# Two attention blocks in fp32 on one core: GpSimd makes two sums of V ahead of its softmax additions

## The chip, the cores and the metric

One NeuronCore of a Trainium2 chip runs the whole program. The metric is the time of one execution on the device in microseconds (us); the median of a few runs is given. A kernel's profile is one further execution under the hardware profiler; its times below are counted from the start of that execution's span.

## The reference

Eight images of 512 channels by 32 x 32 positions pass through two attention blocks, all in float32. Block 0 is a group norm, eight heads of 64 channels, a projection and a residual. Block 1, which the change touches, has one head of 512 channels over 1024 positions:

```python
q = jnp.einsum('oc,bcs->bos', wq, nf) + bq[None, :, None]
k = jnp.einsum('oc,bcs->bos', wk, nf) + bk[None, :, None]
v = jnp.einsum('oc,bcs->bos', wv, nf) + bv[None, :, None]
attn = jnp.einsum('bci,bcj->bij', q, k) * c ** (-0.5)
attn = jax.nn.softmax(attn, axis=-1)
out = jnp.einsum('bcj,bij->bci', v, attn)
out = jnp.einsum('oc,bcs->bos', wo, out) + bo[None, :, None]
return x + out.reshape(b, c, h, w)
```

## The kernel before

The program is one long list of instructions: nothing loops on the chip, and Python unrolls the eight images (`b` = 0 to 7). The order on TensorE (PE), ScalarE (ACT) and VectorE (DVE) is the order of the Python text (`manual_schedule`); the order on GpSimd (POOL) and of the DMAs on SyncE (SP) is chosen by a list scheduler that follows the order of the text as far as operands and buffers let it. Tiles of 128 x 1024 f32 (`tile2`) come from one pool of 36 buffers; a tile takes a buffer that an earlier tile has been done with, and its first writer waits for the last users of that buffer.

Large products are made by Strassen's scheme in Winograd's form. A product of 2 x 2 blocks A and B is done with seven block products of the sums S1 to S4 of A and T1 to T4 of B:

S1 = A21 + A22, S2 = S1 - A11, S3 = A11 - A21, S4 = A12 - S2, and T1 = B12 - B11, T2 = B22 - T1, T3 = B22 - B12, T4 = B21 - T2.

Some block products are themselves split once more in the same way; the tiles named `..._twice` hold the sums of that second step, made by `sums_a` (L477) and `sums_b` (L484).

Block 1 of an image (`attention1`) has these stages on PE:

1. Q (L612), V (L627, L870), with V left in the tiles `c11_v`, `c12_v` (printed as `c_v`).
2. **Phase one of the scores**: `line(0..3)` (L1308) and the split product S1 T1 (L1325).
3. **Phase two of the scores**: the split products A12 B21 and S3 T3, interleaved step by step (L1325). DVE adds each result bank to its tile `p` (L1335, one operand in PSUM and one in SBUF). ACT turns finished tiles into exponentials (L1299). A tile that needs the fifth product gets it by `with_p5` (L1378, DVE, both operands in SBUF, 128 x 1024).
4. **Phase three of the scores**: the split products S4 B22 and A22 T4, in the same way.
5. **The values**: P times V (L1489), in five of seven steps for two groups of channels `c` = 0 and 1, in the order A11, S1, S2, S3, A22; then two split steps (L1619). In the last image all seven steps are whole ones.

The sum of the exponentials over the keys is collected in the tile `acc` by `add_up` (L1294 the first addition, L1296 the others): its half 0 by POOL, its half 1 by DVE. In the values, after the S1 steps, `sums` lets PE multiply both halves of `acc` by ones (L1555); DVE inverts the result (L792), and two small DMAs spread it.

The sums S1 and S2 of V are made by POOL in `sum_v` (L1437): two additions of 128 x 512 each. S3 and S4 of V are made by DVE later. T1 to T4 of P are made by DVE (`finish_values`, L1482, both operands in SBUF). POOL also makes the second-step sums of Q's S4 and A22 (`halve_a`, L477, printed as `S_twice` and `A_twice`), of V's A12 (`halve_v`, L477, `A_v_twice`) and of P's B22 (`halve_p`, L484, `B_p_twice`). In the text, `sum_v(1)` and `sum_v(2)` stand between phase two and phase three.

On DVE the order around the change is: the L1335 additions of phase three, T1 (two instructions), the seven additions of its half of `acc`, T2 (two), S3 of V, T3, the inversion.

Of the kernel before, what the change touches and what calls it, by code (L numbers as in the profile page):

```python
# [65 lines left out]
def two_attention_blocks(  # L66
# [17 lines left out]
    nc = tc.nc  # L84
# [13 lines left out]
    def banks(tag, name):  # L98
        return psum.tile([P, 2, HALF], FP, tag=tag, name=name)

    def tile2(name):
        return tpool.tile([P, 2, HALF], FP, tag="t", name=name)
# [484 lines left out]
    def together(*groups):  # L587

        groups = list(groups)
        spares.clear()  # L590
        while groups:
            for g in list(groups):
                if next(g, g) is g:
                    groups.remove(g)
                else:
                    yield
        spares.clear()

    def at_steps(steps, hooks):

        n = -1
        for n, _ in enumerate(steps):
            for hook in hooks.get(n, []):
                hook()
        assert n >= max(hooks, default=-1)
# [603 lines left out]
    def attention1(xs, norm, b, at_values):  # L1209
# [20 lines left out]
        def halve_a(name, t=None, engine=nc.vector):  # L1230
            q = {f"A{n}": v for n, v in halve(q_parts[name], lambda i, j: (j, i)).items()}
            twice_a[name] = sums_a(q, flat(tile2(f"{name}_twice_{b}")) if t is None else t, engine)
# [55 lines left out]
        def add_up(j, k, i):  # L1288

            engine = nc.vector if i else nc.gpsimd  # L1290
            for u in range(2):
                seen[i].append(ps[j][k][i][:, u, :])
                if len(seen[i]) == 2:
                    engine.tensor_tensor(acc[:, i, :], *seen[i], ALU.add)  # L1294
                elif len(seen[i]) > 2:
                    engine.tensor_tensor(acc[:, i, :], acc[:, i, :], seen[i][-1], ALU.add)  # L1296

        def exp_of(p):
            nc.scalar.activation(p, p, AF.Exp, scale=norm.factor)  # L1299
# [16 lines left out]
        def twice(a, v, tags, i, j, fresh, final):  # L1316

            a, v = twice_a[a], twice_b[v]  # L1320
            line, single = (banks(tag, f"ps_{n}_1_{b}_{i}{j}")[:, 0, :] for tag, n in zip(tags, "ls"))

            def multiply(bank, x, y, start):
                for u in range(2):
                    nc.tensor.matmul(  # L1325
                        bank[:, u * 2 * P : (u + 1) * 2 * P], v[y][:, u * P : (u + 1) * P], a[x],
                        start=start and u == 0, stop=True, skip_group_check=True,
                    )

            def at(r, t):  # L1330
                return ps[j][t][i][:, :, r * 2 * P : (r + 1) * 2 * P]

            def add(bank, r, t):
                bank = bank.rearrange("p (u q) -> p u q", u=2)
                nc.vector.tensor_tensor(at(r, t), bank, at(r, t), ALU.add)  # L1335

            def take(bank, r, t):
                if fresh:
                    nc.scalar.copy(at(r, t), bank.rearrange("p (u q) -> p u q", u=2))
                else:  # L1340
                    add(bank, r, t)

            def done(r, t):
                if final:
                    exp_of(at(r, t))
                    if i == 0 and (r, t) in ((0, 1), (1, 0)):
                        add_up(j, t, i)

            multiply(line, "A11", "B11", True)
            take(line, 0, 0)  # L1350
            yield
            multiply(single, "A12", "B21", True)
            add(single, 0, 0)
            done(0, 0)
            yield
            multiply(line, "S2", "T2", False)
            take(line, 0, 1)
            yield
            multiply(single, "S1", "T1", True)
            take(single, 1, 1)  # L1360
            yield
            multiply(line, "S3", "T3", False)
            add(line, 1, 1)
            done(1, 1)
            yield
            multiply(single, "S4", "B22", False)
            add(single, 0, 1)
            done(0, 1)
            yield
            multiply(line, "A22", "T4", False)  # L1370
            take(line, 1, 0)
            done(1, 0)
            yield

        def with_p5(i, j, k):

            to, other = ps[j][k][i], ps[1][k][1] if i == 0 else ps[0][k][1]
            nc.vector.tensor_tensor(to, to, other, ALU.add)  # L1378

        def c22(k):  # L1380
            with_p5(1, 1, k)
            exp_of(ps[1][k][1])
# [5 lines left out]
        def halve_t3():  # L1388
# [11 lines left out]
        )  # L1400
        halve_a("S4", None, nc.gpsimd)
        halve_a("A22", None, nc.gpsimd)
        at_steps(
            together(
                twice("A12", "B21", "oo", 0, 0, False, True), twice("S3", "T3", "ss", 1, 0, False, False)
            ),
            {3: [lambda: with_p5(0, 1, 1)]},
        )
        c22(0)

        svs = {f"S{n}": tile2(f"s{n}_v_1_{b}") for n in range(1, 5)}
        quarter_v = [
            [[flat(t)[:, i * HALF : (i + 1) * HALF].rearrange("p (u o) -> p u o", u=2) for t in pair]
# [16 lines left out]
        def sum_v(n, engine):  # L1430

            for a, a21 in zip(v_parts, quarter_v[1][1]):
                x, y, op = {
                    1: (a21, a["A22"], ALU.add), 2: (a["S1"], a["A11"], ALU.subtract),
                    3: (a["A11"], a21, ALU.subtract), 4: (a["A12"], a["S2"], ALU.subtract),
                }[n]
                engine.tensor_tensor(a[f"S{n}"], x, y, op)  # L1437


        twice_v, twice_p = {}, {}  # L1440

# [13 lines left out]
            sums = [t[:, i, :].rearrange("p (u q) -> p u q", u=2) for t in ts for i in range(2)]  # L1455
            twice_p[name] = sums_b(q, sums, engine)

        for n in range(1, 3):
            sum_v(n, nc.gpsimd)
        if not last:  # L1460
            halve_v("A12", nc.gpsimd)
        at_steps(
# [202 lines left out]
    with tc.manual_schedule(engines={PE, ACT, DVE}):  # L1665
# [72 lines left out]
        for b in range(B):  # L1738
            if 0 < b < B - 1:
                ahead = [norm0(load_x(b + 1, nc.sync), b + 1)]  # L1740
            xs, norm, qs, ks = layer0(bs, qs, ks, b, ahead[0] if b + 1 < B else None)
            at_values = {}
            if b + 1 < B:

                again, combine_next = ahead[0], Combined(f"again_{b}")

                def load_again():
                    again.xs = load_x(b + 1, nc.sync)

                at_values = {  # L1750
                    2: [load_again], 7: [lambda: again.normed(again.xs, [0], range(NC))],
                    9: [lambda: again.normed(again.xs, [1], range(NC))],
                    10: [lambda: combine_next.take(again.xs)],
                    **{n + 10: [lambda n=n: combine_next.make(n)] for n in range(1, 5)},
                }
                bs = combine_next.parts
            attention1(xs, norm, b, at_values)
# [412 lines left out]
```

## Time and profile before

| | |
|---|---|
| runs | 2862.26, 2857.89, 2862.63 us; median 2862.26 |
| the profiled execution | 2860.0 us, its span 2858.2 us |
| granted TensorE clock, mean | 0.998 |
| PE busy | 2832.0 us (99%) |
| DVE busy | 2141.3 us (75%) |
| ACT busy | 1117.0 us (39%) |
| POOL busy | 282.9 us (10%) in 236 instructions |
| one image | about 352 us |

The span is the time from the first to the last instruction; 1.8 us of the execution lie around it. A busy share is an average over stages that have different limits, and PE's busy time is partly modelled, so what matters for one stage is which wait ends last in it. In the lists of instructions a line gives the start and the duration in us, the engine, the line of the kernel, the operation, the tiles (out<-in) and the shape; xN joins N instructions; in brackets stands the idle time of that engine before it and what ended it. PEld is the weight load that goes ahead of a matmul, PEclk the granted share of PE's full clock.

### The profile page before, as it was taken

To read this page: it belongs to the slowest core of one execution; us is meant where nothing else is said; L and a number is where in the kernel's file an instruction comes from. 1 tells how busy PE (TensorE), PEld (TensorE's weight loads), DVE (VectorE), ACT (ScalarE), POOL (GpSimd) and SP (SyncE) were. 2 spreads that over 40 slices of the span, in tenths; PEclk is the share of its full clock that TensorE was granted. 3 is DMA by queue.
4 is the path that set the end of the run, shared out by engine and by line. 5 is a ranking of instruction groups with operands and counts; after the bars stand their busy time and mean duration, and the time that the engine had idled before them with its cause. 6 is when DMAs were issued, how large, how long until landed. Compare 5 with 4: busy or idle time off the path is not lost.

```text
span 2858.2 us, 38362 instructions
## 1 busy us (share of the span) xinstructions
PE 2832.0 (99%) x15328; PEld 1521.2 (53%) x15328; DVE 2141.3 (75%) x2891; ACT 1117.0 (39%) x1564; POOL 282.9 (10%) x236
## 2 busy tenths in 40 slices
PE   9999999999999999999999999999999999999999
PEld 5434765347643476435763356733567336673365
DVE  6686696867967778776787777777777777767867
ACT  3462324623256232553325522265232642326432
POOL 0000220002100031000400004000040000400012
PEclk9999999999999999999999999999999999999999
DMA  8512132121322212213132131322213222121001
GB/s 287 178 42 74 66 111 93 42 89 53 110 93 49 84 73 93 91 45 107 56 107 76 42 106 56 107 78 47 98 56 107 78 57 87 63 84 58 8 16 38
DMA packets 81227, 228.90 MB, mean 80 GB/s; under 512 B 20080, under 2 KB 20880, under 8 KB 74640
## 3 DMA queue, kind: packets, MB, share of 16 engines
q1 hardware_dynamic: 76576, 210.61, 22.9%
q10 hardware_dynamic: 4464, 15.76, 1.7%
q8 instruction: 122, 2.00, 0.3%
q14 instruction: 65, 0.53, 0.1%
HBM read 157.35 MB, written 30.70 MB: 66 GB/s over the span
## 4 chain that ended last, share of the span: by engine, by line
PE 89%; DVE 9%; SPq 1%; ACT 1%; issue 1%; DMA 0%; POOL 0%; DVEq 0%; POOLq 0%
PE s L921 16%; PE ps_o L940 15%; PE ps_q L612 10%; PE ps_v L627 7%; PE ps_p L612 5%; PE ps_l L1325 5%; PE ps_s L1308 4%; PE ps_s L1325 4%; PE ps_o L1489 3%; PE ps_k L612 3%; PE ps_l_v L627 3%; PE ps_l_qk L849 3%; DVE acc L1296 2%; PE ps_s_v L870 2%; PE ps_s_two L1619 2%; PE ps_s_qk L842 2%
## 5 line engine op out<-in xcount | busy, mean ns | idle before, releaser
L778 ACT ACTIVATE p<-s 128x1024 f32<-128x1024 f32 x512 | 523.6, 1024 | 322.4 <-PE s L921 308.6
L780 DVE TENSOR_TENSOR acc<-acc,p 128x1024 f32<-128x1024 f32 x384 | 469.1, 1222 | 99.5 <-ACT p L778 86.4
L940 PE MATMUL ps_o<-p,v 64*64 64x512 f32 x4096 | 528.7, 589 | 0.0
L940 PEld LDWEIGHTS ps_o<-p,v 64*64 64x64 f32 x4096 | 156.6, 133 | 282.8 <-issue 278.9
L921 PE MATMUL s<-q,k 64*64 64x512 f32 x2304 | 298.5, 591 | 0.0
L921 PE MATMUL s<-c_q,c_k 64*64 64x512 f32 x1792 | 233.0, 590 | 0.0
L339 POOL TENSOR_TENSOR rstd<-rstd,minus_half 128x4 f32<-128x4 f32 (+1 forms) x16 | 19.8, 1239 | 2058.3 <-DVE rstd L338 2058.3
L1489 PE MATMUL ps_o<-t_p,s_v 128*128 128x512 f32 x384 | 171.4, 603 | 4.2 <-ACT held_sum L788 4.2
L921 PEld LDWEIGHTS s<-q,k 64*64 64x64 f32 x2304 | 86.3, 133 | 162.6 <-issue 156.6
L921 PEld LDWEIGHTS s<-c_q,c_k 64*64 64x64 f32 x1792 | 67.7, 133 | 126.3 <-issue 114.9
L780 DVE TENSOR_TENSOR acc<-p,p 128x1024 f32<-128x1024 f32 x64 | 77.8, 1216 | 73.5 <-ACT p L778 73.5
L1299 ACT ACTIVATE p<-p,factor 128x512 f32<-128x512 f32 (+1 forms) x112 | 85.1, 780 | 112.1 <-DVE p L1335 89.6
L1489 PEld LDWEIGHTS ps_o<-t_p,s_v 128*128 128x128 f32 x384 | 73.5, 193 | 98.0 <-issue 85.8
L1313 ACT COPY p<-ps_s 128x512 f32<-128x512 f32 x96 | 53.1, 588 | 178.7 <-PE ps_s L1308 178.7
L1335 DVE TENSOR_TENSOR p<-ps_l,p 128x512 f32<-128x512 f32 x136 | 90.6, 684 | 42.8 <-PE ps_l L1325 41.9
L612 PE MATMUL ps_p<-t_p,w_p 128*128 128x512 f32 x256 | 114.8, 597 | 2.5 <-DVE u_p L1183 1.5
L612 PE MATMUL ps_q<-t,w_wqk 128*128 128x512 f32 x256 | 116.0, 597 | 0.0
L425 ACT COPY u_q<-ps_q 128x512 f32<-128x512 f32 x75 | 43.5, 580 | 177.2 <-PE ps_q L612 177.2
L1066 DVE RECIPROCAL inv<-inv 128x512 f32<-128x512 f32 x28 | 93.7, 3346 | 22.9 <-ACT inv L788 22.9
L425 ACT COPY u_v<-ps_v 128x512 f32<-128x512 f32 x48 | 28.1, 585 | 204.9 <-PE ps_v L627 185.9
L1335 DVE TENSOR_TENSOR p<-ps_s,p 128x512 f32<-128x512 f32 x112 | 74.8, 684 | 41.3 <-PE ps_s L1325 41.3
L627 PE MATMUL ps_v<-w_v,t_again 128*128 128x256 f32 x448 | 99.0, 379 | 0.0
(457 smaller groups left out, 4935.4 us busy)
## 6 DMA issues: line engine op xcount, KB each, us to landing
x<-in_x SPq DMA_DIRECT2D x92, 512.0 KB, 6.8
w_qk<-stored_qk SPq DMA_DIRECT2D x14, 1792.0 KB, 7.2
inv<-inv SPq DMA_DIRECT2D x248, 64.0 KB, 2.0
w_wqk<-stored_wqk SPq DMA_DIRECT2D x8, 1792.0 KB, 7.6
fold<-acc SPq DMA_DIRECT2D x56, 256.0 KB, 3.1
w_wvo<-stored_wvo SPq DMA_DIRECT2D x8, 1792.0 KB, 7.6
out<-x SPq DMA_DIRECT2D x28, 512.0 KB, 3.4
w_v<-stored_v SPq DMA_DIRECT2D x7, 1792.0 KB, 7.1
```

The costliest lines, as they stand in the source:

```text
L612: nc.tensor.matmul(bank, w[a][:, k, c * P : (c + 1) * P], bs[b][:, k, :], start=fresh and k == 0, stop=k == 1, skip_group_check=True,)
L627: nc.tensor.matmul(bank[:, u * 2 * P : (u + 1) * 2 * P], bs[b][:, k, n * P : (n + 1) * P], w[a][:, k, :], start=fresh and u == k == 0, sto ...
L778: nc.scalar.activation(p, s, AF.Exp, scale=factor)
L780: nc.vector.tensor_tensor(acc, first, p, ALU.add)
L849: nc.tensor.matmul(bank, of(i, a)[:, k, :], bs[v][:, k, :], start=start and k == 0, stop=k == 1, skip_group_check=True,)
L921: nc.tensor.matmul(s[cols, j, :], ks[pair][k0 // HALF][rows, k0 % HALF : k0 % HALF + HD], qs[pair][g][rows, :], start=True, stop=True,)
L940: nc.tensor.matmul(o[cols, half, :], vs[kt][rows, c0 : c0 + HD], p[rows, j, :], start=kt == 0, stop=kt == NT - 1,)
L1066: nc.vector.reciprocal(invs[g], invs[g])
L1308: nc.tensor.matmul(bank, bs[v][:, k, t * P : (t + 1) * P], q_parts[a][:, k, :], start=a == "A11" and k == 0, stop=k == 1, skip_group_check ...
L1325: nc.tensor.matmul(bank[:, u * 2 * P : (u + 1) * 2 * P], v[y][:, u * P : (u + 1) * P], a[x], start=start and u == 0, stop=True, skip_group ...
L1335: nc.vector.tensor_tensor(at(r, t), bank, at(r, t), ALU.add)
L1489: nc.tensor.matmul(bank, v_parts[kt // 2][a][:, kt % 2, c * P : (c + 1) * P], p_parts[kt // 2][b][:, kt % 2, cols], start=fresh and kt == ...
```

## The change

The definitions around `sum_v` and the two calls `sum_v(1)`, `sum_v(2)` on GpSimd move from behind phase two to ahead of it. Nothing is computed otherwise, and no instruction is added or removed: 4 GpSimd additions for each image are issued earlier in the text, and the two tiles that they fill take their buffers earlier.

```diff
         halve_a("S4", None, nc.gpsimd)
         halve_a("A22", None, nc.gpsimd)
-        at_steps(
-            together(
-                twice("A12", "B21", "oo", 0, 0, False, True), twice("S3", "T3", "ss", 1, 0, False, False)
-            ),
-            {3: [lambda: with_p5(0, 1, 1)]},
-        )
-        c22(0)
-
         svs = {f"S{n}": tile2(f"s{n}_v_1_{b}") for n in range(1, 5)}
...
                 engine.tensor_tensor(a[f"S{n}"], x, y, op)
 
+        for n in range(1, 3):
+            sum_v(n, nc.gpsimd)
+        at_steps(
+            together(
+                twice("A12", "B21", "oo", 0, 0, False, True), twice("S3", "T3", "ss", 1, 0, False, False)
+            ),
+            {3: [lambda: with_p5(0, 1, 1)]},
+        )
+        c22(0)
+
...
-        for n in range(1, 3):
-            sum_v(n, nc.gpsimd)
         if not last:
             halve_v("A12", nc.gpsimd)
```

## The prediction

> **What bounds the kernel now.** I began with the page: PE is busy 99% of the span, so only a stage where PE waits can give anything. I then took the chain of waits from 360 to 380 us, which is where the moved sums are first used (image 0; the other images show the same at steps of about 352 us).
>
> ```profile
> PE 2832.0 (99%) x15328; PEld 1521.2 (53%) x15328; DVE 2141.3 (75%) x2891; ACT 1117.0 (39%) x1564; POOL 282.9 (10%) x236
> ```
>
> ```profile
> 360.32 1.74 PE ps_l L1325 x8
> ...
> 363.56 3.43 DVE t_p L1482 x2
> 367.00 1.69 DVE acc L1294
> ...
> 375.40 1.65 DVE acc L1296
> ...
> 377.07 0.70 DVE acc L1296
> ...
> 377.82 0.65 PE ps_o L1555 x4
> ```
>
> The chain leaves PE at 362 and runs through DVE until 377.8: T1, then seven additions of 1.65 to 1.69 us, of which only the last takes 0.70. The same addition is slow six times and fast once, so something holds DVE. The instructions of GpSimd and PE in time show what:
>
> ```profile
> 337.55 1.71 POOL L477 TENSOR_TENSOR A_twice<-q,A_twice 128x256 f32<-128x256 f32 x1
> 348.84 1.27 POOL L1294 TENSOR_TENSOR acc<-p 128x512 f32<-128x512 f32 x1 [9.58 <-ACT p L1299]
> 350.07 3.49 POOL L1437 TENSOR_TENSOR s_v<-c_v,c_v 128x512 f32<-128x512 f32 x2
> 353.51 3.57 POOL L1437 TENSOR_TENSOR s_v<-s_v,c_v 128x512 f32<-128x512 f32 x2
> ...
> 369.76 6.73 POOL L1296 TENSOR_TENSOR acc<-acc,p 128x512 f32<-128x512 f32 x4
> ```
>
> ```profile
> 376.54 0.62 PE L1555 MATMUL ps_o<-acc,ones 128*32 128x256 f32 x4 [0.77 <-POOL acc L1296]
> 377.82 0.62 PE L1555 MATMUL ps_o<-acc,ones 128*32 128x256 f32 x4 [0.65 <-DVE acc L1296]
> 379.05 15.67 PE L1489 MATMUL ps_o<-t_p,s_v 128*128 128x512 f32 x32 [0.60 <-ACT held_sum L788]
> ```
>
> POOL stands idle for 9.58 us, then works without a break from 348.84 to 376.49, and DVE becomes fast when POOL stops. PE ends its S1 steps near 375.62 and starts S2 at 379.05: 3.43 us. It waits for POOL's half of acc, for DVE's half, and then for T2. The last wait is put down to ACT, but S2 reads no result of held_sum, and T2's first half on DVE ended at 378.90, so I read it as T2. The last image has no such wait and prices the stage without it:
>
> ```profile
> 2820.89 0.64 PE L1555 MATMUL ps_o<-acc,ones 128*32 128x256 f32 x8
> 2821.45 17.43 PE L1489 MATMUL ps_o<-t_p,s_v 128*128 128x512 f32 x40
> ```
>
> There the chain gives L1555 0.57 us. So 3.43 - 0.57 = **2.86 us of PE idle in each of seven images**, 20.0 us together. The table of stretches adds one thing: behind the idle time PE sometimes gets a lower clock.
>
> ```profile
> 379.00:383.00 4.00, 3.96 (x6) 1.67 (x7) 4.00 (x5) 0.00 (x0) 0.00 (x0) 0.57 0.00 0
> 1083.20:1086.60 3.40, 3.35 (x8) 1.63 (x9) 3.40 (x5) 0.00 (x0) 0.00 (x0) 1.00 0.02 5
> ```
>
> PEclk (third column from the right) is 0.57 in image 0, near 0.55 in image 1, and 1.00 in images 2 to 6. At 0.57, 4.00 us lose 1.7 us; two images make 3.4 us.
>
> **What the Trainium skill says.** "SBUF — State Buffer", Who interferes with whom: a DVE instruction with two SBUF inputs and a GpSimd instruction that reads SBUF lock each other out for a whole instruction; with one SBUF input DVE doesn't contend. The trace agrees: L1335 (PSUM and SBUF) takes 0.69 us beside busy and idle POOL alike, while L1378 (two SBUF inputs) takes
>
> ```profile
> 341.88 1.22 DVE L1378 TENSOR_TENSOR p<-p,p 128x1024 f32<-128x1024 f32 x1
> 350.63 1.79 DVE L1378 TENSOR_TENSOR p<-p,p 128x1024 f32<-128x1024 f32 x1
> ```
>
> 1.22 us with POOL idle and 1.79 us where a sum of V had begun at 350.07 and ended at 351.33: it waited for that end. "TensorE: Matmul & The Clock Gate", Part 1: an idle window of about 3.4 us halves PE's clock for about another, the windows running free of the program; two images of seven agree. "Perfetto Trace Analysis", GPSIMD Engine Instruction: time GpSimd by start-to-start spacing; two uncontended additions here give 350.07 - 348.84 = 1.23 us, and I use 1.24.
>
> **The change, part by part.** No instruction is added, and none of those moved is a DMA. SP's queue is not passed: its loads of x start when phase three's last matmuls free buffers. On POOL, four additions pass the acc additions.
>
> *Removed from 350 to 357:* the four sums hold POOL 3.49 + 3.57 = 7.06 us there, 4 x 1.24 = 4.96 of their own and 2.1 of waiting for two L1378.
>
> *Added from 339:* the halvings end at 339.25. S1 and S2 need V, complete before phase one, and buffers; phase one's last matmul starts before 338, so its buffers are free. They run S1 339.2 to 341.7, S2's first half to 342.95. DVE's L1378 arrives at 341.88 and waits 1.07 us. Behind it stand four L1335. The bank that PE reuses at 344.5 was read by 343.69, and would be read by 344.8: PE loses about 0.5 us (**A**). The backlog is caught up by about 347, because an L1335 takes 0.6 us and PE offers one in 0.86. S2's second half ends at 345.4, before the first acc addition at 348.84, so the sums themselves cost POOL's other work nothing.
>
> *The next two L1378* (350.63 and 354.73). Before, the first waited 0.58 us and the second none. Now POOL has its acc additions or A_v_twice there. The first waits for between a 0.7 us and a 1.27 us instruction: -0.1 to +0.6 us against before (**B**). The second may meet A_v_twice or an addition: 0 to 0.7 us (**C**). PE has no slack at either: its load at 353.13 waited for the L1335 behind the first. A + B + C is 0.4 to 1.8 us; I take D = 1.2.
>
> *The acc stage, shifted by D.* POOL now waits for ACT instead: B_p_twice needs the exponentials that ended at 357.13, so runs about 358.4 to 363.4; the last four acc additions begin there instead of at 369.76. They take 4 x 1.24 with T1's two instructions and one DVE addition let in between (1.2 + 1.2 + 0.6): end near 371.3, not 376.49. DVE: T1 ends near 369.4 (before 367.0; PE needs its halves at about 370 and 371.7), one addition is held, six take 0.72 each, end near 375.6, not 377.76. T2's first half is ready at 376.8, not 378.90. PE ends S1 at 375.62 + 1.2 = 376.8, does the acc products in 0.57 and starts S2 at 377.4 instead of 379.05. **Gain 2.86 - 1.2 = 1.66 us an image.** DVE has only 0.6 us left there: it is the next thing to be late. Behind S2, the DVE work for S3 and A22 is released by PE and ACT, so it moves along; before the two split steps PE waits 0.15 us now and should again.
>
> *Last image:* no wait to remove, and without next-image tiles its sums may run in phase one, so B alone: +0.5 us.
>
> *Sum:* 7 x 1.66 = 11.6, less 0.5, plus 3.4 for two low-clock windows no longer opened: 14.5 us. The profiled execution's 2860.0 becomes 2845.5 (span 2843.7). It stands 2.26 us below the median of the runs, 2862.26, so the forecast is **2848 us**. Bounds: D = 0.4 gives 7 x 2.46 + 3.4 = 20.6, so 2842; D = 1.8 with DVE 0.5 us late and no low-clock saving gives 7 x 0.56 - 0.5 = 3.4, so 2859.
>
> **The rivals.**
> *The collisions eat the gain* (16%). For it: PE has no slack at B and C, and POOL works gaplessly there still. Against: the collision was there before too, at 350.63. With D near 2.5 the gain is 0.4 us an image, 2.5 us: 2860.
> *Slower: the buffers are not free in phase two* (14%). The pool is tight: the halvings of S4 waited for a buffer until 332.75. If S1's buffer is one that phase two's matmuls release near 349.7, the in-order queue puts the first acc addition behind the sums instead of ahead. POOL's last addition then ends 1.24 us later, and sums and S2 with it: 7 x 1.24 = 8.7 us, 2871. It decides when the buffer's release lies behind 348.84; against it, phase one leaves Q's S1 and S2 and x's T1 and T2 unused. Three full collisions, 3 x 1.24 = 3.7 against 2.86, end on this side as well.
> *The order on POOL stays* (3%): the scheduler left POOL idle for 9.58 us with the sums possible. Then 2862.
>
> **How the numbers follow.** About 0.2% (5.7 us) is what a measurement of this kernel can tell from no change. Forecast 67%, all but the very end of its range faster; so faster 0.67, same 0.18 (second and fourth rival, less a little), slower 0.15. The range runs from 2838, somewhat below the D = 0.4 bound since more than two windows may have been slow in the median run, to 2864, which takes in the second and last rivals; the slower case is left out.
>
> **What would show it.** Right: s_v at 339.2 to 345.4, ahead of acc; L1378 near 341.9 at about 2.3 us; POOL's last acc addition near 371; DVE's last five or six additions near 0.7 us; L1555 as x8 without a wait between; S2 1 to 2.5 us earlier, PEclk 1.00 behind it. Wrong: s_v behind 348; PE gaps of a microsecond in phases two and three; or T2 still ending later than L1555.

## The result, and the profile after

| | before | changed |
|---|---|---|
| runs, side by side | 2857.89 to 2863.33 us, 6 runs | 2839.17 to 2842.84 us, 6 runs |
| median | 2860.27 us | **2840.30 us** |
| ratio, 95% interval | | 0.9931 [0.9918, 0.9944] |
| the profiled execution, its span | 2860.0, 2858.2 us | 2839.93, 2838.1 us |

The change saves 20 us (0.7%). The forecast was 2848 us, faster: the direction and the mechanism held. It had put the gain at 14.3 us, from a median of 2862.26 us; the measured time lies 7.7 us below the forecast.

Two lines of the page of the changed kernel, the busy time and the chain's shares by engine:

```profile
PE 2825.0 (100%) x15328; PEld 1518.4 (53%) x15328; DVE 2124.3 (75%) x2891; ACT 1118.0 (39%) x1564; POOL 273.6 (10%) x236
PE 91%; DVE 6%; issue 1%; SPq 1%; DMA 0%; ACT 0%; POOL 0%; DVEq 0%; POOLq 0%
```

The chain's shares before were these:

```profile
PE 89%; DVE 9%; SPq 1%; ACT 1%; issue 1%; DMA 0%; POOL 0%; DVEq 0%; POOLq 0%
```

DVE had 9% of the chain before and has 6% now: 3% of 2838 us is some 85 us of chain that no longer leaves PE, far more than the 20 us gained. The chain's share says where the path runs, not what is lost on it. The chain of waits itself, image 0, from 355 us (start, us, what):

```profile
354.80 2.02 DVE p L1378
356.82 0.61 DVE p L1335
357.43 0.04 issue
357.47 1.99 PE ps_l L1325 x8
...
362.92 13.73 PE ps_o L1489 x32
376.65 0.57 PE ps_o L1555 x8
377.22 7.08 PE ps_o L1489 x16
```

Before, the chain left PE at 362 and ran through DVE to 377.8. Now it stays on PE through T1, the additions, L1555 and S2: L1555 is one block of eight, 0.57 us, without a wait. What is new is the first line: in phase three the path passes through a DVE instruction, L1378. The instructions of POOL in time say why both are so (start, us, engine, line, operation, in brackets the idle time before):

```profile
337.82 1.71 POOL L477 TENSOR_TENSOR A_twice<-q,A_twice 128x256 f32<-128x256 f32 x1
339.48 2.50 POOL L1429 TENSOR_TENSOR s_v<-c_v,c_v 128x512 f32<-128x512 f32 x2
341.94 3.49 POOL L1429 TENSOR_TENSOR s_v<-s_v,c_v 128x512 f32<-128x512 f32 x2
349.37 1.27 POOL L1294 TENSOR_TENSOR acc<-p 128x512 f32<-128x512 f32 x1 [3.94 <-ACT p L1299]
...
354.46 3.50 POOL L1296 TENSOR_TENSOR acc<-acc,p 128x512 f32<-128x512 f32 x2
...
362.97 7.04 POOL L1296 TENSOR_TENSOR acc<-acc,p 128x512 f32<-128x512 f32 x4
```

The sums of V (now L1429) fill 339.5 to 345.4, inside what was 9.58 us of idle time, and POOL's last addition to acc ends at 370.01 instead of 376.49. And DVE beside it:

```profile
342.15 2.15 DVE L1378 TENSOR_TENSOR p<-p,p 128x1024 f32<-128x1024 f32 x1
...
351.17 1.25 DVE L1378 TENSOR_TENSOR p<-p,p 128x1024 f32<-128x1024 f32 x1
...
354.73 2.09 DVE L1378 TENSOR_TENSOR p<-p,p 128x1024 f32<-128x1024 f32 x1
...
370.60 4.33 DVE L1296 TENSOR_TENSOR acc<-acc,p 128x512 f32<-128x512 f32 x6
374.84 2.35 DVE L1482 TENSOR_TENSOR t_p<-p,t_p 128x1024 f32<-128x1024 f32 x2
```

The same in the kernel before, where the prediction has not shown it:

```profile
354.73 1.21 DVE L1378 TENSOR_TENSOR p<-p,p 128x1024 f32<-128x1024 f32 x1
...
368.70 9.06 DVE L1296 TENSOR_TENSOR acc<-acc,p 128x512 f32<-128x512 f32 x6
377.68 2.35 DVE L1482 TENSOR_TENSOR t_p<-p,t_p 128x1024 f32<-128x1024 f32 x2
```

The six L1296 took 9.06 us together before and take 4.33 now, 0.72 each: POOL has stopped. T2's first half ends at 376.06 and PE asks for it at 377.15. The price stands in the three L1378: 2.15, 1.25 and 2.09 us against 1.22, 1.79 and 1.21 before.

All images can be read from the starts of PE's matmuls. Three stretches of an image are enough:

| us | before | changed |
|---|---|---|
| phases two and three (first matmul of phase two to the first L1489) | 20.81 to 20.82 | 21.41 to 21.44, in image 1 21.16 |
| of the values: S1's first matmul to S2's | 10.28 to 10.30 | 7.53 |
| the values up to the first L1619 | 38.13 to 38.15 at full clock | 35.40 to 35.41 |

The table has images 0 to 6. Each gains 2.72 us in the values, pays 0.6 in the phases (0.34 in image 1) and so wins 2.1 (2.4): 15.1 us for the seven.

The table of stretches behind the former wait (bounds, us, PE busy and its matmuls, PEclk, DMA share, GB/s), changed kernel, image 0:

```profile
377.20:380.60 3.40, 3.40 (x12) 1.00 0.02 5
```

PEclk is 1.00; before it was 0.57 here.

### The profile page after: what moved, and what is told of

Read it like the earlier page. It is cut to its first block, busy times and chain, and to the rows that moved or that the text cites. A ratio compares the mean times of both kernels' runs of the same rounds, so it can differ in the third digit from the quotient of the medians.

```text
span 2838.1 us, 38370 instructions
## 1 busy us (share of the span) xinstructions
PE 2825.0 (100%) x15328; PEld 1518.4 (53%) x15328; DVE 2124.3 (75%) x2891; ACT 1118.0 (39%) x1564; POOL 273.6 (10%) x236
## 4 chain that ended last, share of the span: by engine, by line
PE 91%; DVE 6%; issue 1%; SPq 1%; DMA 0%; ACT 0%; POOL 0%; DVEq 0%; POOLq 0%
PE s L921 16%; PE ps_o L940 15%; PE ps_q L612 10%; PE ps_v L627 7%; PE ps_o L1489 7%; PE ps_p L612 5%; PE ps_l L1325 4%; PE ps_s L1308 4%; PE ps_k L612 3%; PE ps_l_v L627 3%; PE ps_s L1325 3%; PE ps_l_qk L849 3%; PE ps_s_v L870 2%; PE ps_s_two L1619 2%; PE ps_s_qk L842 2%; PE ps_o_v L870 1%
## 5 line engine op out<-in xcount | busy, mean ns | idle before, releaser
L1489 PE MATMUL ps_o<-t_p,s_v 128*128 128x512 f32 x384 | 168.2, 594 | 0.0
L1489 PEld LDWEIGHTS ps_o<-t_p,s_v 128*128 128x128 f32 x384 | 72.3, 190 | 91.3 <-issue 89.2
```

The source lines that it names most:

```text
L1489: nc.tensor.matmul(bank, v_parts[kt // 2][a][:, kt % 2, c * P : (c + 1) * P], p_parts[kt // 2][b][:, kt % 2, cols], start=fresh and kt == ...
```

## The experiments

**The theory.** PE waited for T2, and T2 was late because DVE's additions to acc were held up by POOL's, each by about 0.95 us (1.65 instead of 0.70), as long as POOL read SBUF. The change lets POOL stop 6.5 us sooner. What it gives back comes from L1378, which now meets POOL's reads in phases two and three. **The rivals:** PE waited only for POOL's own half of acc, or S1 and S2 of V were themselves late; a POOL that is busy at all slows DVE; PE's last wait was ACT's copy of the sums, as the profile wrote; the low clock behind the idle time was the whole loss.

In the variants the numbers of lines behind an insertion are shifted by two or four (L1482 appears as L1484 or L1486, L1555 as L1557), and the clock of the span by up to 1.1 us.

### Reads on GpSimd put back behind acc

```diff
             {3: [lambda: c22(1)], 5: [] if last else [lambda: halve_p("B22", nc.gpsimd)]},
         )
+        for op in [ALU.subtract, ALU.add] * 2:
+            nc.gpsimd.tensor_tensor(acc[:, 0, :], acc[:, 0, :], ps[0][0][0][:, 0, :], op)
```

> The changed kernel with four additions more on GpSimd behind its last one: acc's first half minus one part of p and plus it again, twice, so that acc is the same but for rounding. GpSimd then reads SBUF until near 376.8 instead of 370.0, as long as before the change, though S1 and S2 are made early. My theory (GpSimd's reads hold up DVE): four more of DVE's additions take about 1.65 instead of 0.69, T2's first half ends near 379.9 instead of 376.06, PE waits 2.5 to 3 us ahead of S2 in each of seven images, and the gain is gone: 2858 to 2864. Of this at most 0.3 us an image is GpSimd's own half of acc, late at 376.8 for PE's 376.6. Rival, what counted was that S1 and S2 are ready early, or GpSimd's half of acc: 2840 to 2843. Rival, the low clock alone: 2840 to 2845.

Measured: 2865.05 us (2864.24 to 2867.32, 8 runs) against 2859.36 for the kernel before, ratio 1.0023 [1.0012, 1.0033]: the gain is gone and 5.7 us with it, since the price at the L1378 stays and the last image loses too. POOL in this variant, and the chain of waits:

```profile
363.87 7.04 POOL L1296 TENSOR_TENSOR acc<-acc,p 128x512 f32<-128x512 f32 x4
370.99 6.60 POOL L1469 TENSOR_TENSOR acc<-acc,p 128x512 f32<-128x512 f32 x4
```

```profile
371.50 1.65 DVE acc L1296
...
373.17 1.65 DVE acc L1296
...
374.84 1.65 DVE acc L1296
...
376.51 1.65 DVE acc L1296
...
378.18 0.70 DVE acc L1296
...
378.91 0.70 DVE acc L1296
379.61 0.04 issue
379.65 0.65 PE ps_o L1557 x4
```

Four reads more on POOL, four slow additions more on DVE, and the fifth is fast again as soon as POOL is done at 377.6. S1 and S2 of V are as early as in the changed kernel, so their readiness was not what counted. POOL's own half of acc costs 0.15 us here (PE's step to the first L1557 took 1.10 us instead of 0.95); DVE's half and T2 cost the other 2.7, for PE takes 10.33 to 10.37 us from S1 to S2 where the changed kernel takes 7.53. The last image, which had no such wait, loses 2.0 us as well: there S1 waits for DVE's reading of a PSUM bank (L1504), which stands behind the slow additions (a step of 2.77 us between weight loads ahead of S1, where 0.43 is usual). This the forecast had left out.

The run also answers the rival of the low clock. The stretches behind the wait, images 0, 1 and 2 (images 3 to 6 read the same):

```profile
380.60:384.00 3.40, 3.12 (x8) 1.00 0.02 5
731.70:735.10 3.40, 3.12 (x8) 1.00 0.02 5
1082.80:1086.20 3.40, 3.10 (x8) 1.00 0.02 5
```

PE waited as long as before in each of seven images and kept its full clock behind all of them, and the span was 2863.1 us all the same. The low clock comes on top; it is not the loss. (This profile has one low clock, elsewhere: behind the gap in the last image that is told of below.)

### Writes alone in the same place

```diff
+        idle = bias_q.rearrange("p c n -> p (c n)")
+        nc.gpsimd.tensor_tensor(idle[:, :1], acc[:, 0, :1], acc[:, 0, :1], ALU.add)
+        for n in range(25):
+            nc.gpsimd.memset(idle, 0.0)
```

> The changed kernel with about 5 us more on GpSimd behind its last addition to acc, but without reads: 25 memsets of a dead constant tile, held behind acc by one addition of a single column. My theory (it is the reading of SBUF by both that excludes, not a busy GpSimd): DVE's additions stay at 0.69 to 0.75 us and the time at 2840 +- 2. Rival, a busy GpSimd slows DVE whatever it does: DVE's additions 1.2 us and more there, 2848 to 2860.

Measured on the same chip: 2842.10 us (2841.57 to 2842.65), ratio 0.9942 [0.9926, 0.9959], which overlaps the changed kernel's interval and lies 0.1 us above the expected range. POOL and DVE:

```profile
371.35 6.49 POOL L1471 MEMSET many_bias_q<- 128x128 f32 x25
```

```profile
371.28 4.32 DVE L1296 TENSOR_TENSOR acc<-acc,p 128x512 f32<-128x512 f32 x6
```

POOL is as busy as in the variant with reads, 6.49 us against 6.60, over DVE's additions; DVE takes 0.72 us for each of them. The wait does not come back: from S1 to S2 PE takes 7.53 us in all seven images, as in the changed kernel. So a busy POOL alone costs nothing here. Of the two kinds of work, the one that reads SBUF slows DVE; whether a read of another kind than an addition would do it was not tried. The Trainium skill, "SBUF — State Buffer", Who interferes with whom, says just this of a two-input DVE instruction (it contends with a GpSimd instruction that reads SBUF, "not with one that only writes it"), and this pair of runs agrees: 1.65 us beside reads, 0.72 beside writes.

### Half of the move

```diff
-        for n in range(1, 3):
-            sum_v(n, nc.gpsimd)
+        sum_v(1, nc.gpsimd)
...
+        sum_v(2, nc.gpsimd)
         if not last:
             halve_v("A12", nc.gpsimd)
```

> The changed kernel with only S1 of V ahead of phase two; S2 stays where it was before the change, behind the first addition for the softmax. My theory (what counts is when GpSimd's last addition to acc ends, because DVE's additions are slow until then): GpSimd ends about 3.3 us sooner than in the kernel before instead of 6.5, near 373 on the clock of image 0. DVE then has two slow additions fewer (1.65 to 0.69), 2 x 0.96 = 1.9 us, and T2's first half ends near 377.0 instead of 378.90. PE is there near 376.3, so it still waits about 0.7 of the 2.86 us. The collision in phase two (0.27 us of PE) is gone, since one sum ends before L1378 comes. Gain 1.7 to 2.2 us an image and 0 to 5 us of low clock: 2842 to 2848. Rival, each sum is worth half: 2850. Rival, only a full removal helps: 2858 to 2860.

Measured on the same chip: 2843.17 us (2842.69 to 2844.88), ratio 0.9947 [0.9931, 0.9964]. DVE and PE:

```profile
370.96 6.21 DVE L1296 TENSOR_TENSOR acc<-acc,p 128x512 f32<-128x512 f32 x6
```

```profile
376.93 0.93 PE L1555 MATMUL ps_o<-acc,ones 128*32 128x256 f32 x8
378.46 5.82 PE L1489 MATMUL ps_o<-t_p,s_v 128*128 128x512 f32 x13 [0.60 <-ACT held_sum L788]
```

Two of the six additions are still slow (2 x 1.65 + 4 x 0.72 = 6.2), and PE still waits: 0.3 us inside L1555 (0.93 us for the eight, where the changed kernel takes 0.64) and 0.64 ahead of S2, where the step between the weight loads of L1555 and S2 is 1.16 us against 0.52. Together it is 0.95 us in each of seven images (8.47 to 8.49 from S1 to S2 against 7.53); expected were 0.7. So the sums aren't worth half each: by medians against the same runs of before (2859.36), half of the move brought 16.2 us and the whole one with harmless writes behind it 17.3. The second half removes the last 0.95 us of the wait and pays for about half of it with the two collisions, which this variant does not have: its L1378 take 1.22, 1.79 and 1.28 us, and its phases two and three 20.88 to 20.90 us instead of 21.41. By the traces that leaves some 3 us between half and whole; the medians show 1.1, from few runs whose intervals overlap.

### Which wait was the last

```diff
-        invs, later = [], []
+        invs, later, later_held = [], [], []
...
-            held(ps, f"sum_1_{b}")
+            if last:
+                held(ps, f"sum_1_{b}")
+            else:
+                later_held.append(ps)
...
+        hooks[5].append(lambda: held(later_held[0], f"sum_1_{b}"))
```

This is the kernel before, with the copy of the sums taken later.

> The kernel before with ACT's copy of the softmax sums (held_sum) taken two hooks later in all but the last image. The trace of before put PE's last wait ahead of S2 (0.60 us to 379.05) down to this copy; I read it as T2 on DVE. My theory: S2 still starts 3.4 us after S1's end, right behind T2's first half, and the wait is put down to DVE: 2860 +- 2. Rival, PE did wait for the copy: S2 starts 0.5 to 0.6 us sooner, 7 x 0.55 = 3.9 us: 2856.

Measured: 2858.30 us (2855.49 to 2862.78, 12 runs), ratio 1.0000 [0.9992, 1.0009]. PE:

```profile
378.95 0.62 PE L1555 MATMUL ps_o<-acc,ones 128*32 128x256 f32 x4 [0.65 <-DVE acc L1296]
380.18 4.10 PE L1489 MATMUL ps_o<-t_p,s_v 128*128 128x512 f32 x9 [0.60 <-DVE t_p L1482]
```

The wait is the same 0.60 us and now carries its true name, DVE's T2; from S1 to S2 PE takes the same 10.28 to 10.29 us. ACT's copy had merely ended later than T2 and been taken for it.

### The price: three edits at the L1378

The changed kernel once more and three variants of it, all on one chip. The first takes phase three's L1378 one hook sooner; the second does that and takes phase two's five hooks later, into POOL's idle stretch; the third leaves both and moves POOL's four A_v_twice (`halve_v`, with its definition) ahead of phase two as well.

> The changed kernel itself, for the comparison with the three beside it: 2840 to 2842.

```diff
-            {3: [lambda: c22(1)], 5: [] if last else [lambda: halve_p("B22", nc.gpsimd)]},
+            {2: [lambda: c22(1)], 5: [] if last else [lambda: halve_p("B22", nc.gpsimd)]},
```

> The changed kernel with DVE's L1378 of phase three (c22(1)) one hook sooner. It stood behind a GpSimd addition from 354.73 to 356.82, and PE lost 0.44 us there by the trace. One hook sooner it stands behind a half of A_v_twice that ends near 354.5, 0.7 us long and not 1.24. My theory (PE has no slack at these places, each wait of L1378 is paid): PE waits 0 to 0.15 us there and 7 or 8 x 0.3 to 0.44 us is won: 2837 to 2839, 2 to 3.5 us below the changed kernel on the same chip. Rival, this wait is made up later, since PE waits there for DVE or ACT anyway: equal to the changed kernel within 1 us.

```diff
-            {3: [lambda: with_p5(0, 1, 1)]},
+            {8: [lambda: with_p5(0, 1, 1)]},
...
-            {3: [lambda: c22(1)], 5: [] if last else [lambda: halve_p("B22", nc.gpsimd)]},
+            {2: [lambda: c22(1)], 5: [] if last else [lambda: halve_p("B22", nc.gpsimd)]},
```

> The same, and L1378 of phase two (with_p5(0, 1, 1)) five hooks later as well, into GpSimd's idle stretch from 345.4 to 349.4, so that no sum of V holds it. My theory: both collisions are gone, 0.27 + 0.44 us of PE an image, 4 to 5.5 us in all: 2835 to 2837. Rival, the collisions cost nothing in the end: equal to the changed kernel within 1 us. Rival, at the later place L1378 holds up phase two's last reads of PSUM with less time to catch up: 1 to 4 us slower than the variant with phase three alone.

```diff
...
         for n in range(1, 3):
             sum_v(n, nc.gpsimd)
+        if not last:
+            halve_v("A12", nc.gpsimd)
...
-        if not last:
-            halve_v("A12", nc.gpsimd)
```

> The changed kernel with A_v_twice ahead of phase two too (four 128x256 additions on GpSimd, 2.8 us, right behind the sums of V), so that GpSimd stops about 2.8 us sooner still. My theory (nothing is left to win at the acc stage, where PE no longer waits; only DVE's collisions count): DVE's last additions are faster by nothing that PE sees, GpSimd's first additions to acc now stand at 350.6 to 353 and hold L1378 of 351.17 by up to 1.2 us where it was held by none, and the one of 354.73 is free: 0 to +0.4 us an image, 2840 to 2844. Rival, every microsecond by which GpSimd stops sooner is worth about 0.3 us an image, as from before to after (2.1 for 6.5): 2.8 x 0.33 x 7 = 6.4 us, 2834.

| | us, median of 5 (range) | ratio to before |
|---|---|---|
| before, same chip, 9 runs | 2859.42 (2856.04 to 2862.68) | |
| changed kernel again | 2839.99 (2839.76 to 2840.70) | 0.9931 [0.9918, 0.9945] |
| phase three's L1378 sooner | 2838.08 (2837.14 to 2839.64) | 0.9926 [0.9912, 0.9939] |
| and phase two's later | **2836.22** (2834.71 to 2838.17) | 0.9920 [0.9906, 0.9933] |
| A_v_twice early | 2837.70 (2836.70 to 2837.93) | 0.9922 [0.9908, 0.9935] |

DVE in the second variant, the three L1378 of image 0:

```profile
346.39 1.22 DVE L1378 TENSOR_TENSOR p<-p,p 128x1024 f32<-128x1024 f32 x1
...
350.83 1.22 DVE L1378 TENSOR_TENSOR p<-p,p 128x1024 f32<-128x1024 f32 x1
...
353.77 1.34 DVE L1378 TENSOR_TENSOR p<-p,p 128x1024 f32<-128x1024 f32 x1
```

All three are free, or nearly. In the changed kernel two steps between PE's weight loads in these phases took 0.58 and 0.76 us where the others take 0.22, and the step behind each took 0.11: 0.26 and 0.44 us lost (0.58 + 0.11 - 0.43, 0.76 + 0.11 - 0.43). The first variant has only the first of them, the second has neither. Phases two and three take 21.41 us in the changed kernel, 21.05 in the first variant and 20.72 in the second. In image 1 the collision of phase two is missing already in the changed kernel and the first variant (21.16, 20.78), and in both variants the last image loses 0.43 us (20.72 to 21.15), since its L1378 now meets a POOL addition (1.85 us). So the traces give the first variant 6 x 0.36 + 0.38 - 0.43 = 2.1 us and the second 6 x 0.33 + 0.06 = 2.0 more; the medians show 1.9 and 1.9. What PE loses at the L1378 is paid in full in the time, and removing it makes the best version here, 23 us below the kernel before.

The third variant missed both forecasts (2840 to 2844 and 2834). POOL and DVE:

```profile
351.38 3.72 POOL L1296 TENSOR_TENSOR acc<-acc,p 128x512 f32<-128x512 f32 x2 [0.52 <-ACT p L1299]
```

```profile
351.38 1.23 DVE L1378 TENSOR_TENSOR p<-p,p 128x1024 f32<-128x1024 f32 x1
...
354.91 1.27 DVE L1378 TENSOR_TENSOR p<-p,p 128x1024 f32<-128x1024 f32 x1
```

I had expected the L1378 of 351.4 to stand behind POOL's addition. The two records start within 2 ns of each other, DVE's first, and it is POOL that waits: two additions in 3.72 us instead of 2.5. The later L1378 is free too, so phase three's 0.44 us is gone (the two phases take 20.98 us), and the time is the first variant's within 0.4 us. POOL stops 1.8 us sooner than in that one and T2 is ready a microsecond sooner, and nothing comes of it: at the acc stage there was nothing left to win.

## Why the prediction was right in its sign and short in its size

**The wait and its cause: right.** POOL's end was forecast at 371.3 (370.01), five or six fast additions of 0.72 us (six), S2 1 to 2.5 us sooner (379.05 to 377.15, 1.9), the sums at 339.2 to 345.4 (339.48 to 345.43). All of the wait went. Its size was 2.76 us and not 2.86 (10.29 - 7.53 in every image): the forecast took S1's end at 375.62, but from S1's last matmul to the first L1555 PE takes 0.52 us even where nothing waits, 0.09 more than the 0.43 between others. The variants with reads and with writes show the cause; the later copy confirms the reading of the last wait as T2.

**The failed step is D, what the collisions give back: 1.2 us taken, 0.6 measured** (21.41 - 20.82). By its three places:

- *A*, phase two: 0.5 us taken, 0.26 measured. L1378 waited 0.93 us (2.15 for 1.22), a little less than the forecast 1.07. The bank's last read ended at 344.90, and PE's weight load and matmul both stand at 344.95, with the next step after 0.11 us instead of 0.22; I had counted 0.2 us for a weight load behind the read. Image 1 is a test of this term: its L1378 met no sum (1.27 us), and its two phases took 0.25 us less than the others'.
- *B*, -0.1 to 0.6: the low end. The 351.17 instruction took 1.25 us, behind only the tail of an A_v_twice; before, it had waited 0.58 for a sum of V. PE gained about 0.1.
- *C*, 0 to 0.7: 0.44, behind an acc addition, within the range given.

D is 0.26 - 0.1 + 0.44 = 0.6, and 2.72 - 0.6 = 2.1 us an image where 1.66 stood. Image 0 shows it: S2 is 1.9 us sooner although PE entered phase two 0.27 us later. The seven images win 15.1 us and not 11.6, so the forecast is short by 3.5. D alone makes 4.5 of this (6 x 0.6, and 0.86 in image 1), and the wait, taken too large, gives 1.0 back (7 x 0.14). That D is paid one for one was right: the variants without the collisions win it back.

**Low clock: two windows taken, three in the profile.** I had looked at the stretches behind the wait alone. The last image of the kernel before has one more, behind another idle gap of PE (2.57 us between two weight loads of V, at 2748.3):

```profile
2750.80:2754.20 3.40, 3.31 (x10) 0.65 0.01 2
```

The changed kernel has the same gap, at 2730.15, and keeps its full clock behind it. So 3.4 should have been 5.1 us, but the third window has nothing to do with the change: all ten traces of this study have that gap, and two of them a low clock behind it (the kernel before, and the changed one with reads put back). The runs show how much such windows weigh. Every run's mean granted clock is known to three digits, and the times of the kernel before, 28 runs on two chips, follow it:

| mean clock | runs | us |
|---|---|---|
| 1.000 | 3 | 2855.32 to 2856.04 |
| 0.999 | 13 | 2856.54 to 2859.92 |
| 0.998 | 12 | 2859.49 to 2862.68 |

One window of 3.4 us at half clock loses 1.7 us and lowers the mean by 0.0006, so by this estimate the three rows are no window, one or two, and three or four. The changed kernel spreads less (2839.76 to 2840.70 in five runs, 2839.17 to 2842.84 in six others). The fastest runs of the two are 16.2 us apart; 15.1 of this is the waits, and the other 1.1 stays open. In the two profiles 5.1 of the 20.1 us are low clock. No run set the number of windows: that the missing wait is what makes them fewer is argued, not shown.

**The last image: -0.5 taken, nothing measured.** From its predecessor's first L1619 to the end of the span it takes 347.98 and 348.05 us in two profiles of the changed kernel and 348.01 in the kernel before where that had no low clock (the variant with the later copy). There L1378 came first, as in the third variant above (1.23 us).

**The sum.** 15.1 + 5.1 = 20.2, measured on the two profiled spans 20.1. Of the forecast's 5.6 us error on the profiled execution, 3.5 are D less the wait's excess, 1.7 the third window and 0.5 the last image, less 0.1 left over. The third window was luck for the changed kernel. The other 2 us of the distance from 2848 come from the median it was tied to: three runs gave 2862.26, six gave 2860.27.

**The rivals.** Collisions near 2.5 us an image did not come; three full ones would have needed each L1378 to wait 1.24 us and PE to pay it all. The buffers were free, and the sums went ahead of acc in every image.

## What to carry to other kernels

GpSimd, working without a break beside DVE, set DVE's pace here while both read SBUF: look for one DVE instruction that is slow several times and fast once, and for the engine that stopped in between. Move such work into a stretch where most of DVE's instructions have only one SBUF operand, and then look at each two-operand instruction that lies in the new stretch: it pays there, and a few hooks sooner or later in the text can take that back. Half of such a move can bring most of the gain, as it did here (16.2 of 17.3 us), because the gain ends where PE no longer waits while the collisions go on.

## What the runs showed of the hardware

- GpSimd's memsets, which only write, left DVE alone: six 128x512 additions took 4.32 us beside 25 memsets, 4.33 without them.
- Side by side without a break, a 128x512 addition of DVE and one of GpSimd took 1.67 us from one start to the next (DVE at 370.38, 372.05, 373.73 in the kernel before). One after the other they would take 0.73 + 1.24 = 1.97, so by these steps the two exclude each other for less than both whole instructions; the prediction had spoken of a whole one.
- Started within 2 ns of each other (351.38), DVE's 128x1024 instruction, the first of the two, took 1.23 us; the pair of GpSimd additions took 3.72 instead of 2.5.
- Seven waits of PE of 2.8 us, each broken by two sets of four short matmuls, left the clock at 1.00 behind them in one execution (reads put back); in another (the kernel before) two of seven were followed by 3.4 us at half clock, in a third (the later copy) one of seven. The gap of 2.57 us in the last image was followed by a low clock in two of ten. The Trainium skill, "TensorE: Matmul & The Clock Gate", Part 1, has the window run free of the program; these runs fit that, since the same waits met a low clock in one execution and not in another. They also show that a gap of 2.57 us, shorter than the idle window of about 3.4 us that the prediction took from that page, can be followed by a low clock.
